# Patch-scan layer: part of the B products by ScalarE and TensorE, step sizes spread from DRAM, some C products on GpSimd

## The chip, the cores and the metric

The kernel runs on one core of a Trainium2 chip. All data are float32. The metric is the device time of one execution in microseconds. The core has a matrix engine (PE, with its weight loads shown apart as PEld), a vector engine (DVE), an activation engine (ACT), a general engine (POOL) and a queue that issues most of the transfers (SP). Each has its own list of instructions and works through it in order; they wait for one another by semaphores. Tiles lie in the on-chip memory SBUF or in PSUM, where PE writes its results; DRAM is off the chip.

## The reference

Four layers with residuals act on x of shape (8, 96, 64, 64). The change is in layer 2, a selective scan over patches. Cut to its core:

```python
xin, z = split(in_proj_w @ x)                 # 192 channels each
x_s = bilinear_sample(xin, ref + tanh(off2(gelu(bn(conv3x3(xin))))))
xt = patches of 4 x 4 pixels, L = 16 steps each
xs4 = [xt, xt turned, both reversed]          # 4 directions
dts, Bs, Cs = x_proj_weight @ xs4             # per direction; N = 16 states
delta = softplus(dt_projs @ dts + bias)
h[d, n] = h[d, n] * exp(delta[d] * A[d, n]) + delta[d] * u[d] * B[n]   # per step
y[d] = sum over n of h[d, n] * C[n]
y = layernorm(sum of the four directions + D * u) * silu(z)
x = x + out_proj_w @ y
```

Each channel d has 16 states n, so a recurrence runs for 192 x 16 rows, in each of four directions, over all pixels.

## The kernel before

**Tiling.** An image of 64 x 64 pixels is worked in eight chunks of 512 pixels (32 patches of 16 steps); eight images make 64 chunks. In a chunk, each of the four directions (in `ORDER`, index n = 0 to 3; n odd is a reversed one) has 12 groups: six sets of 32 channels, and two parts each. A group holds 32 channels x 4 states on 128 partitions, twice (two sets of states side by side), 1024 columns. So a chunk is 48 groups, and the layer 3072. Directions 0, 1 and 2, 3 form two pairs, which share one chain for delta.

**What one group needs** (class `WideSlots`, `slot`):
- L458: SP spreads delta and delta*u of 32 channels over 128 partitions, into a tile `dd` (512 KB). One spread serves the two parts. Before, it reads the SBUF tile `delta`, each channel's row going to four neighbouring partitions (`p = 4 * channel + state`).
- L466: ACT makes two exps of 512 columns, exp(delta * A), into the PSUM tile `ps_d` (`g.da`; three buffers).
- L485: POOL multiplies delta*u by B (`brep`) into the SBUF tile `dbu` (eight buffers): the B product, 1024 columns.
- L1584 (`scan`): DVE runs the recurrence over 1024 columns, from `ps_d` and `dbu` into `ps_d`.
- L490: DVE multiplies the states by C (`crep`) into `dbu`: the C product. A group listed in `LATE2` would have its scan write `dbu` and its C product done by POOL; the list is empty.
- L373 (`total`): PE sums over the states with a matrix of ones (`k_red2`), two matmuls of 512 columns (four instructions).

**Order.** The order on each engine is written out by hand, slot by slot: slot t holds scan t, the exps of group t+1, the C product of t-1, the B product of t+2, the sum of t-2 and the spread of t+6. Around these stand "side" instructions, put in a slot by `sl.at(slot, engine, run)`; "first" is ACT's place just after the exps, "act" its later place in the slot. A chunk begins at slot B, the next at B + 48, so the slots below are often given modulo 48. A pair begins at T = B or B + 24. Side work of a chunk begins 100 slots ahead of B: load, normalise, 3 x 3 convolution (18 taps), gelu, offsets, tanh, bilinear sampling on POOL (`lines` to `sampled`), the projections for u and for B and C, the softplus chain for delta (`pair`: L1495 to L1513 on ACT, L1522 to L1538 on POOL, 24 products of 512 columns per chunk), copies that mark the patch edges (`edges`, L1546). Behind the groups come centring, variance, gate (`gated`), output projection, residual, store (`end`, `gates`). All side matmuls share one PSUM tile, `ps_a`, which ACT empties before the next may begin.

Gelu (L1312), tanh (L1341) and silu (L1469) each need a table load on ACT, and one more to get back to the tables of exp and ln.

Of the kernel before, what the change touches and what calls it, by code (L numbers as in the profile page):

```python
# [13 lines left out]
ALU = mybir.AluOpType  # L14
# [43 lines left out]
def shape_constants():  # L58
# [19 lines left out]
    for d in range(GC2):  # L78
        red[d * HS2 : (d + 1) * HS2, 64 + d] = 1.0
# [33 lines left out]
def lay_out(i):  # L113
# [16 lines left out]
    for k in range(4):  # L130
# [28 lines left out]
        .transpose(2, 3, 0, 1, 4)  # L159
# [84 lines left out]
LOG_EXP = "natural_log_exp_and_others"  # L244
FAR = 1e25
AHEAD = 4
AHEAD2, SPREAD2 = 6, 4
LATE2 = ()
# [193 lines left out]
class WideSlots(Slots):  # L442


    def run(self):
        ts = list(self.plan) + [t + d for t in self.groups for d in (-self.ahead, 3)]
        with self.S.tc.manual_schedule():
            for t in range(min(ts), max(ts) + 1):
                self.slot(t)

    def slot(self, t):
# [4 lines left out]
        elif g:  # L456
# [3 lines left out]
                g.steps().unsqueeze(1).to_broadcast([self.gc, 128 // self.gc, 2 * NW]),  # L460
            )
        g = G(t + 1)
        if g:
            g.da = new(self.psd, [128, 2, NW], "ps_d")
            for i in range(2):
                nc.scalar.activation(  # L466
                    g.da[:, i, :], g.dd[:, 0, :], AF.Exp, scale=g.a[:, i : i + 1]
                )
        self.side(t, "first")
        g = G(t)  # L470
        if g:
            g.h = g.dbu if g.late else g.da
            g.scan(*(v.rearrange("p i l -> p (i l)") for v in (g.h, g.da, g.dbu)))
# [4 lines left out]
        g = G(t - 3)  # L478
# [4 lines left out]
        if g:  # L483
            g.dbu = new(self.pool, [128, 2, NW], "dbu", bufs=8)
            nc.gpsimd.tensor_tensor(  # L485
                g.dbu, g.dd[:, 1:2, :].to_broadcast([128, 2, NW]), g.b(), ALU.mult
            )
        g = G(t - 1)
        if g:
            (nc.gpsimd if g.late else nc.vector).tensor_tensor(g.dbu, g.h, g.c(), ALU.mult)  # L490
        for engine in ("pool", "dve", "sp", "end"):
# [698 lines left out]
def layer2(S, src, dst, st_in, st_out, images, cp, W, ready, finish):  # L1190
# [3 lines left out]
    with ExitStack() as ctx:  # L1194
# [32 lines left out]
        for k in range(4):  # L1227
# [3 lines left out]
        for k in range(2):  # L1231
            t = new(cp, [CH + 1, 2, NW], f"xs{k}")
# [11 lines left out]
        def front(ch, b, pad, xs, c, B):  # L1244
# [4 lines left out]
            def load():  # L1249
                ch["x"] = new(fp, [CH, 10 * IW], "xl")  # L1250
# [50 lines left out]
            for m, slots, last in (  # L1301
                (0, ((-81, 1), (-80, 2), (-79, 1), (-78, 1), (-77, 1), (-76, 1), (-75, 2)), -74),
                (1, ((-67, 1), (-66, 2), (-65, 1), (-64, 1), (-63, 1), (-62, 1), (-61, 2)), -60),
# [7 lines left out]
            def gelu():  # L1311
                nc.scalar.activation(ch["t"], ch["t"], AF.Gelu)  # L1312
                nc.scalar.preload_act_table_set(LOG_EXP)

            sl.at(B - 60, "act", gelu)

            def offset(a):
# [16 lines left out]
                sl.at(B - 59 + a, "pe", pe)  # L1334
                sl.at(B - 58 + a, "first", act)
# [4 lines left out]
            def tanh():  # L1340
                nc.scalar.activation(ch["f"], ch["f"], AF.Tanh)  # L1341
                nc.scalar.preload_act_table_set(LOG_EXP)

            def place():
# [3 lines left out]
                nc.scalar.activation(f, f, AF.Identity, bias=sl.half[:CH], scale=0.5)  # L1348

            sl.at(B - 57, "act", tanh)  # L1350
            sl.at(B - 56, "act", place)

# [28 lines left out]
            def sampled():  # L1381
                for k in range(2):
                    nc.gpsimd.tensor_tensor(
                        xs[:CH, 0, k * 256 : (k + 1) * 256].rearrange("p (n h w) -> p n h w", h=4, w=4),
# [11 lines left out]
            sl.at(B - 44, "act", lambda: nc.scalar.copy(xs[:CH, 1, :], turned(xs[:CH, 0, :])))  # L1396

            def inner(j):


                def pe():
# [4 lines left out]
                        xs[:CH, 0, :],  # L1406
# [9 lines left out]
                sl.at(B - 23 + j, "pe", pe)  # L1416
                sl.at(B - 22 + j, "first", act)
# [4 lines left out]
            def both():  # L1422
                ch["pa"] = new(psa, [128, NW], "ps_a")
                for o in range(2):
                    nc.tensor.matmul(
                        ch["pa"], bc_w[:, o].rearrange("c m s -> c (m s)"), xs[:CH, o, :],
                        start=o == 0, stop=o == 1,
                    )

            def both_out():  # L1430
                ch["bc"] = new(fp, [128, NW], "bc")
# [5 lines left out]

            sl.at(B - 20, "pe", both)
            sl.at(B - 19, "first", both_out)
            sl.at(B - 19, "sp", both_store)  # L1440

        def gates(ch, pad, T):
            x = pad[:, 1:9, 1 : IW + 1]

            def gate(m):
# [16 lines left out]
                sl.at(T + m, "pe", pe)  # L1462
                sl.at(T + 1 + m, "first", act)
# [8 lines left out]
            sl.at(T + 2, "act", silu)  # L1472

        def pair(ch, xs, n, T):
# [4 lines left out]
            def first(j):  # L1479
                def pe():  # L1480
# [5 lines left out]
                        xs[:, n, :],  # L1486
# [752 lines left out]
```

## Time and profile before

| what | us |
| --- | --- |
| median of 17 runs (18056.6 to 18186.87) | 18152.37 |
| the profiled execution | 18125.05 |
| its span, first to last instruction | 18123.2 |
| first and last scan of the patch layer, from the span's start | 3875.4, 14309.9 |

| engine | busy us in the span | share |
| --- | --- | --- |
| DVE | 16212.3 | 89% |
| POOL | 14803.3 | 82% |
| PE | 13711.7 | 76% |
| ACT | 10061.2 | 56% |

The span holds four layers: layer 0 to about 3050 us, layer 1 to about 3870, the patch layer to about 14310, layer 3 after it. Shares over the whole span mix them. Busy times are sums of the instructions' records; consecutive records of an engine overlap by about 0.1 us, so the distance from start to start is what adds up to time.

### The profile page before, as it was taken

The page shows a single profiled execution, that of the slowest core. Times are in us where ns is not written, and L with a number is a line of the kernel's source. Part 1 is how long each engine was busy: PE and PEld are TensorE (multiplying, and loading weights), DVE is VectorE, ACT ScalarE, POOL GpSimd, SP SyncE. Part 2 cuts the span into 40 slices and gives each one's busy share as a digit, 9 for nine tenths or more (in the row PEclk, how much of TensorE's full clock was granted, in tenths as well). Part 3 has the DMA queues.
Part 4 walks back from the last instruction along what each step waited for, and adds up shares of the span by engine and source line. Part 5 has one row for each costly group of instructions (what it writes and reads, how often), then busy time and mean ns, then how long its engine had stood idle before and what let it go on. Part 6 is the DMA issues. An engine that isn't in the chain of part 4 may idle for free. (4 is left out here: it accounts for less than half of the span.)

```text
span 18123.2 us, 125849 instructions
## 1 busy us (share of the span) xinstructions
PE 13711.7 (76%) x32964; PEld 4902.4 (27%) x32964; DVE 16212.3 (89%) x11111; ACT 10061.2 (56%) x16056; POOL 14803.3 (82%) x8876
## 2 busy tenths in 40 slices
PE   8999998968888888888888888888888644444433
PEld 2323223722222222222222222222222111111111
DVE  7999998679999999999999999999999766777667
ACT  6777775556666666666666666666666311111110
POOL 7999996059999999999999999999999656666555
PEclk8999998989999999999999999999999866666666
DMA  7888887366665666666566666656565444544444
GB/s 125 148 149 149 149 149 120 65 153 137 132 138 131 139 130 137 134 134 137 132 138 131 138 131 137 134 134 137 132 138 130 119 130 142 151 143 143 138 127 121
DMA packets 802719, 2437.25 MB, mean 134 GB/s; under 512 B 259123, under 2 KB 260864, under 8 KB 734830
## 3 DMA queue, kind: packets, MB, share of 16 engines
q1 hardware_dynamic: 654541, 1976.06, 52.3%
q0 software_dynamic: 147456, 453.13, 8.3%
q8 instruction: 262, 4.29, 0.1%
q14 instruction: 460, 3.76, 0.1%
HBM read 1116.39 MB, written 104.46 MB: 67 GB/s over the span
## 5 line engine op out<-in xcount | busy, mean ns | idle before, releaser
L373 PE MATMUL ps_y<-dbu,k_red 128*96 128x512 f32 x15360 | 7603.6, 620 | 1472.9 <-DVE dbu L490 1424.8
L485 POOL TENSOR_TENSOR dbu<-dd,brep 128x1024 f32<-128x1024 f32 x3072 | 7212.0, 2359 | 222.9 <-PE ps_y L373 105.9
L1584 DVE TENSOR_TENSOR_SCAN ps_d<-ps_d,dbu 128x1024 f32<-128x1024 f32 x3072 | 7015.7, 2284 | 126.9 <-issue 106.9
L466 ACT ACTIVATE ps_d<-dd,l_alog 128x512 f32<-128x512 f32 x6144 | 4241.6, 691 | 3353.0 <-DVE dbu L490 3236.4
L373 PEld LDWEIGHTS ps_y<-dbu,k_red 128*96 128x96 f32 x15360 | 2346.4, 166 | 6373.2 <-DVE dbu L490 3380.7
L490 DVE TENSOR_TENSOR dbu<-ps_d,crep 128x1024 f32<-128x1024 f32 x3072 | 3702.3, 1205 | 0.0
L2073 POOL DMA_INDIRECT v<-t,idx x2304 | 2191.9, 951 | 1541.5 <-DVE s L2100 705.1
L2100 DVE TENSOR_REDUCE s<-v 128x864 f32<-128x3456 f32 x256 | 1553.6, 6069 | 445.5 <-remote 236.6
L355 POOL TENSOR_TENSOR dbu<-dd,brep 128x1024 f32<-128x1024 f32 x768 | 1794.5, 2355 | 164.4 <-DMA dd<-delta 145.4
L2091 DVE TENSOR_TENSOR v<-v,ps_w 128x3456 f32<-128x3456 f32 x256 | 958.4, 3744 | 656.0 <-ACT ps_w L2083 584.7
L735 DVE TENSOR_TENSOR_SCAN ps_d<-ps_d,carry,dbu 128x512 f32<-128x512 f32 x1184 | 1452.8, 1272 | 96.4 <-POOL dbu L355 75.9
L1280 PE MATMUL ps_a<-pad,woff 96*96 96x512 f32 x2304 | 1146.5, 598 | 26.6 <-ACT pad L1257 24.1
L2119 ACT COPY smp<-ps_t 128x768 f32<-128x768 f32 (+1 forms) x512 | 244.5, 529 | 1659.1 <-remote 947.3
L337 ACT ACTIVATE ps_d<-dd,l_alog 128x512 f32<-128x512 f32 x1536 | 999.6, 682 | 182.7 <-DMA dd<-delta 126.3
L2111 PE MATMUL ps_t<-k_ident,s 128*128 128x128 f32 (+1 forms) x1792 | 326.9, 334 | 965.1 <-issue 571.6
L365 DVE TENSOR_TENSOR dbu<-ps_d,crep 128x512 f32<-128x512 f32 x1344 | 850.6, 674 | 0.0
L1522 POOL TENSOR_TENSOR sp_m<-sp_m,sp_s 128x512 f32<-128x512 f32 x384 | 487.8, 1271 | 371.8 <-ACT sp_s L1510 371.8
L1908 PE MATMUL ps_a<-xpad,l_om 96*27 96x512 f32 x1152 | 605.3, 674 | 53.8 <-issue 53.6
L1925 PE MATMUL ps_u<-k_ident,oc 27*128 27x27 f32 x256 | 32.8, 251 | 697.2 <-ACT oc L1920 577.6
L1280 PEld LDWEIGHTS ps_a<-pad,woff 96*96 96x96 f32 x2304 | 373.8, 164 | 668.0 <-issue 551.8
L2142 PE MATMUL ps_o<-smp,l_w 128*96 128x512 f32 (+1 forms) x896 | 477.6, 692 | 97.8 <-ACT smp L2119 91.8
L2111 PEld LDWEIGHTS ps_t<-k_ident,s 128*128 128x128 f32 (+1 forms) x1792 | 252.5, 170 | 1094.5 <-issue 875.8
(278 smaller groups left out, 15916.8 us busy)
## 6 DMA issues: line engine op xcount, KB each, us to landing
dd<-delta SPq DMA_DIRECT2D x2304, 512.0 KB
brep<-bcd SPq DMA_DIRECT2D x256, 1024.0 KB
crep<-bcd SPq DMA_DIRECT2D x256, 1024.0 KB
v<-t,idx POOLq DMA_INDIRECT x2304
xo<-x SPq DMA_DIRECT2D x128, 192.0 KB
x<-xo SPq DMA_DIRECT2D x128, 192.0 KB
bcd<-bc SPq DMA_DIRECT2D x64, 256.0 KB
xn<-x SPq DMA_DIRECT2D x64, 192.0 KB
```

The source lines that it names most:

```text
L337: nc.scalar.activation(da, g.dd[:, 0, :], AF.Exp, scale=g.a[:, i : i + 1])
L355: nc.gpsimd.tensor_tensor(g.dbu, g.dd[:, 1:2, :].to_broadcast([128, 2, NW]), g.b(), ALU.mult)
L373: self.S.nc.tensor.matmul(y, self.red[:, HD - self.gc * (g.n + 1) : 2 * HD - self.gc * (g.n + 1)], g.dbu[:, i, :], start=first and i == 0, ...
L466: nc.scalar.activation(g.da[:, i, :], g.dd[:, 0, :], AF.Exp, scale=g.a[:, i : i + 1])
L485: nc.gpsimd.tensor_tensor(g.dbu, g.dd[:, 1:2, :].to_broadcast([128, 2, NW]), g.b(), ALU.mult)
L490: (nc.gpsimd if g.late else nc.vector).tensor_tensor(g.dbu, g.h, g.c(), ALU.mult)
L735: nc.vector.tensor_tensor_scan(out, da, dbu, carry[:, n + i : n + i + 1] if c else 0.0, ALU.mult, ALU.add)
L1280: nc.tensor.matmul(ch["pk"][:HD, :], woff[:, k, m * HD : (m + 1) * HD], pad[:, dy : dy + 8, dx : dx + IW], start=k == 0, stop=k == KT - 1,)
L1584: nc.vector.tensor_tensor_scan(out[:, way], da[:, way], dbu[:, way], 0.0, ALU.mult, ALU.add)
L2073: nc.gpsimd.indirect_dma_start(out=st["v"][:, k].rearrange("p q c -> p (q c)"), out_offset=None, in_=flat, in_offset=bass.IndirectOffsetOn ...
L2091: nc.vector.tensor_tensor(v3, v3, ps_w[:, g % 2, j * 4 * KT : (j + 1) * 4 * KT] .unsqueeze(2) .to_broadcast([128, 4 * KT, CH]), ALU.mult,)
L2100: nc.vector.tensor_reduce(st["s"], st["v"].rearrange("p k q c -> p k c q"), mybir.AxisListType.X, ALU.add,)
```

## The change

1. **Layout.** The partition of a group becomes `p = 32 * state + channel` ("state by channel"): `k_red2`, `l2_alog`, the spreads of dd, brep and crep follow it.
2. **Delta through DRAM.** The tile delta | delta*u of a pair is stored in a DRAM tile `dud` in three parts (slots T-12, T-11, T-8), and the spreads read from there. `delta` has one buffer instead of two, and the tile `sp_m` is gone.
3. **B products by ScalarE.** For the groups of part 1 of each odd n (12 of 48), the second 512 columns of the B product are made in another way: delta*u is transposed by PE (`rows`, 16 transposes per chunk and pair together), so that the steps lie on partitions; B is transposed too (`over`, four); ACT multiplies by B as a scale column (`scaled`, 16 x 192 columns per pair); and PE transposes the products back into the second half of `ps_d`, four per group (`turn_of`). The exp that would have gone there goes to `dbu`, the POOL product is 512 columns, and the scan is two scans of 512.
4. **Late groups.** `LATE2` names five of the 48 groups; their C product is POOL's. It moves to slot t+2, the sum to t+4; all other side work of POOL now stands before it.
5. **Slots.** Side work is moved to make room: the projections for u and B, C earlier, the softplus chain three to four slots earlier, the output projection ten earlier; silu seven slots after its first gate matmul instead of two. Tanh uses a table set with exp and tanh (`EXP_TANH`), which saves one table load per chunk. The gates of the last chunk come at B + 50 instead of B + 42.
6. **Tiles.** Three `pad` buffers instead of four; the turned copy of `xs` is gone (matmuls read it turned); `bc` and `xo` share the buffer of `xl`.

The counts of instructions per chunk, before and after: scans of 1024 columns 48 and 36, of 512 columns 0 and 24; C products on DVE 48 and 43; B products of 1024 columns 48 and 36, of 512 columns 0 and 12; transposes 0 and 68; scalings 0 and 32; table loads 6 and 5; spreads of dd 24 and 24; stores to `dud` 0 and 6.

```diff
-LATE2 = ()
+LATE2 = (15, 18, 20, 38, 40)
...
-                g.steps().unsqueeze(1).to_broadcast([self.gc, 128 // self.gc, 2 * NW]),
+                g.steps().unsqueeze(0).to_broadcast([128 // self.gc, self.gc, 2 * NW]),
...
             for i in range(2):
-                nc.scalar.activation(
-                    g.da[:, i, :], g.dd[:, 0, :], AF.Exp, scale=g.a[:, i : i + 1]
-                )
+                da = g.dbu if g.turn and i else g.da
+                nc.scalar.activation(da[:, i, :], g.dd[:, 0, :], AF.Exp, scale=g.a[:, i : i + 1])
+            if g.turn:
+                g.turn(g.da[:, 1, :])
...
-            g.scan(*(v.rearrange("p i l -> p (i l)") for v in (g.h, g.da, g.dbu)))
+            if g.turn:
+                g.scan(g.h[:, 0, :], g.da[:, 0, :], g.dbu[:, 0, :])
+                g.scan(g.h[:, 1, :], g.dbu[:, 1, :], g.da[:, 1, :])
+            else:
+                g.scan(*(v.rearrange("p i l -> p (i l)") for v in (g.h, g.da, g.dbu)))
...
-        g = G(t - 3)
+        g = G(t - 4)
         if g and g.late:
             self.total(g)
...
+            n = 1 if g.turn else 2
             nc.gpsimd.tensor_tensor(
-                g.dbu, g.dd[:, 1:2, :].to_broadcast([128, 2, NW]), g.b(), ALU.mult
+                g.dbu[:, :n, :], g.dd[:, 1:2, :].to_broadcast([128, n, NW]), g.b()[:, :n, :],
+                ALU.mult,
             )
+        self.side(t, "pool")
+        g = G(t - 2)
+        if g and g.late:
+            nc.gpsimd.tensor_tensor(g.dbu, g.h, g.c(), ALU.mult)
         g = G(t - 1)
-        if g:
-            (nc.gpsimd if g.late else nc.vector).tensor_tensor(g.dbu, g.h, g.c(), ALU.mult)
+        if g and not g.late:
+            nc.vector.tensor_tensor(g.dbu, g.h, g.c(), ALU.mult)
...
-            sl.at(B - 60, "act", gelu)
+            sl.at(B - 58, "act", gelu)
...
+            def over():
+                ch["pa"] = new(psa, [128, NW], "ps_a")
+                for k in range(4):
+                    at = slice(k * 128, (k + 1) * 128)
+                    nc.tensor.transpose(ch["pa"][:, at], ch["bc"][:, at], S.ident)
...
-            sl.at(T + 2, "act", silu)
+            sl.at(T + 7, "act", silu)
...
+                def store():
+                    if j == 0:
+                        pr["rows"] = new(dp, [BLK * 128, 2 * NW], "dud")
+                    nc.sync.dma_start(
+                        pr["rows"][j * 128 : (j + 1) * 128],
+                        pr["d"][:, j].rearrange("p x l -> p (x l)"),
+                    )
+
+                sl.at(T - (12, 11, 8)[j], "act", edges)
+                sl.at(T - (12, 11, 8)[j], "sp", store)
...
+            def scaled(m):
+                def run():
+                    if m == 0:
+                        pr["prod"] = new(fp, [128, 4, 6, HS2, GC2], "prod")
+                    k, q = m // HS2, m % HS2
+                    nc.scalar.activation(
+                        pr["prod"][:, k, :, q, :],
+                        pr["du"][:, k, :].rearrange("p (g c) -> p g c", c=GC2),
+                        AF.Copy,
+                        scale=ch["bt"][:, k, n, q : q + 1],
+                    )
+
+                return run
+
+            m = 0
+            for t, count in (
+                (
+                    (-7, 2), (-4, 2), (-3, 2), (-2, 1), (-1, 1), (0, 1), (2, 1), (3, 3), (4, 1),
+                    (5, 2),
+                ),
+                ((-7, 3), (-6, 3), (-5, 3), (-4, 1), (-3, 1), (-2, 1), (3, 2), (4, 2)),
+            )[n]:
+                for _ in range(count):
+                    sl.at(T + t, "act", scaled(m))
+                    m += 1
...
+            def turn_of(h, g):
+                def run(out):
+                    for k in range(4):
+                        nc.tensor.transpose(
+                            out[:, k * 128 : (k + 1) * 128],
+                            pr["prod"][:, k, 3 * h + g].rearrange("p s c -> p (s c)"),
+                            S.ident,
+                        )
+
+                return run
...
+                        turn=turn_of(h, g) if n % 2 and part else None,
...
-                gates(ch, pad, B + (42 if b == images[-1] and c == NC - 1 else 61))
+                gates(ch, pad, B + 50)
```

## The prediction

> **What bounds the kernel now.** I read four views in this order: busy time by stretch (where does the changed layer lie, and which engine is full in it), the groups by line (what one slot costs), the timeline of one slot (how instructions overlap), and the list of waits (where the full engine still loses time).
>
> Busy time in 6 ms from the middle of the patch layer; the columns are length, then busy time and instruction count of PE, PEld, DVE, ACT and POOL, then granted clock, DMA share, GB/s:
>
> ```profile
> core 0: us, PE busy (x) PEld busy (x) DVE busy (x) ACT busy (x) POOL busy (x), PEclk, DMA share, GB/s
> 6000.00:12000.00 6000.00, 5068.12 (x10995) 1686.34 (x10994) 5934.81 (x3609) 4041.86 (x5826) 5651.76 (x3067) 0.99 0.60 134
> 1000.00:2500.00 1500.00, 1388.93 (x2894) 447.84 (x2892) 1429.33 (x1628) 1082.25 (x2163) 1392.11 (x611) 0.95 0.89 149
> ```
>
> DVE is busy 98.9%, POOL 94.2%, PE 84.5%, ACT 67.4%. The reader is to see that DVE sets the pace and that POOL is next.
>
> Groups by line, with shapes kept apart (busy us, mean ns | idle before):
>
> ```profile
> L373 PE MATMUL ps_y<-dbu,k_red 128*96 128x512 f32 x15360 | 7603.6, 620 | 1472.9 <-DVE dbu L490 1424.8 <-DVE dbu L365 34.1 <-POOL dbu L360 4.4
> L485 POOL TENSOR_TENSOR dbu<-dd,brep 128x1024 f32<-128x1024 f32 x3072 | 7212.0, 2359 | 222.9 <-PE ps_y L373 105.9 <-DMA dd<-delta 98.2 <-DVE ps_d L1584 14.2
> L1584 DVE TENSOR_TENSOR_SCAN ps_d<-ps_d,dbu 128x1024 f32<-128x1024 f32 x3072 | 7015.7, 2284 | 126.9 <-issue 106.9 <-POOL dbu L485 17.3
> L490 DVE TENSOR_TENSOR dbu<-ps_d,crep 128x1024 f32<-128x1024 f32 x3072 | 3702.3, 1205 | 0.0
> L735 DVE TENSOR_TENSOR_SCAN ps_d<-ps_d,carry,dbu 128x512 f32<-128x512 f32 x1184 | 1452.8, 1272 | 96.4 <-POOL dbu L355 75.9 <-ACT ps_d L337 16.5 <-ACT carry L744 2.1
> ...
> L1522 POOL TENSOR_TENSOR sp_m<-sp_m,sp_s 128x512 f32<-128x512 f32 x384 | 487.8, 1271 | 371.8 <-ACT sp_s L1510 371.8
> ...
> L735 DVE TENSOR_TENSOR_SCAN ps_d<-ps_d,dbu 128x512 f32<-128x512 f32 x160 | 186.5, 1210 | 94.1 <-POOL dbu L355 86.9 <-ACT ps_d L337 6.9
> ```
>
> A slot is one scan (2284) and one C product (1205) on DVE, one B product (2359) on POOL. The two L735 lines, from layer 0, show what half a scan costs.
>
> Timeline of DVE and of ACT where DVE stops (start us, length, then what; the bracket is idle time before):
>
> ```profile
> 9057.44 2.29 DVE L1584 TENSOR_TENSOR_SCAN ps_d<-ps_d,dbu 128x1024 f32<-128x1024 f32 x1
> 9059.63 1.21 DVE L490 TENSOR_TENSOR dbu<-ps_d,crep 128x1024 f32<-128x1024 f32 x1
> 9061.54 2.30 DVE L1584 TENSOR_TENSOR_SCAN ps_d<-ps_d,dbu 128x1024 f32<-128x1024 f32 x1 [0.70 <-issue]
> 9063.75 1.21 DVE L490 TENSOR_TENSOR dbu<-ps_d,crep 128x1024 f32<-128x1024 f32 x1
> ```
> ```profile
> 9055.60 0.76 ACT L1294 ACTIVATE off<-ps_a,sh,sc 96x512 f32<-96x512 f32 x1
> 9056.37 1.28 ACT L1312 ACT_TABLE_LOAD   x1
> 9057.67 1.06 ACT L1312 ACTIVATE off<-off 96x1024 f32<-96x1024 f32 x1
> 9058.74 1.28 ACT L1313 ACT_TABLE_LOAD   x1
> 9060.04 1.41 ACT L466 ACTIVATE ps_d<-dd,l_alog 128x512 f32<-128x512 f32 x2
> ```
>
> Start to start a scan takes 2.19 us and a product 1.125 us, so an undisturbed slot is 3.315 us. The stop of 0.70 us is called "issue", but ACT's exps for that scan ended just before it: behind gelu and its two table loads (3.67 us) they came late. Tanh and silu each stop DVE for 0.51 us in the same manner in this chunk. Over the layer the "issue" time of L1584 is 106.9/64 = 1.67 us per chunk.
>
> POOL's waits in the same 6 ms (total us, times, longest):
>
> ```profile
> POOL sp_m L1522 <- ACT sp_s L1510: 200.1, 69, 3.8
> POOL dbu L485 <- PE ps_y L373: 57.3, 63, 1.0
> POOL dbu L485 <- DMA dd<-delta: 56.0, 55, 2.0
> ```
>
> L1584's own view gives first and last start as 3875.4 and 14309.9 us: 10434 us for 64 chunks of 48 slots, 163.0 us a chunk. From the rows: 48 x 3.315 = 159.1, one gating product (1.12) and one statistic (0.60), 1.67 stops; sum 162.5, 0.5 short.
>
> **The change, per chunk, on DVE.** (a) Five late groups: their C product leaves DVE, 5 x 1.125 = -5.63 us. No bound is needed, the row is the instruction itself. (b) Twelve scans of 1024 become 24 of 512. No half scan without a carry operand in this layer is shown; layer 0's takes 1.210 (1.12 start to start, with the overlap of 0.09 seen above): 12 x (2.24 - 2.19) = +0.6. Upper bound, the carry form 1.272 (1.18): 12 x 0.17 = +2.0. Lower bound zero. I take +0.6, since the new scans have no carry. That one factor comes from PSUM and one from the product tile in either half, as now, is why I leave the rate alone. (c) The stops. Tanh shares a table set with exp now, so one table load goes (1.28 us) and its 3.67 us become 1.06 in one slot and 2.4 in the next: no stop. Silu moves three slots from its gate copy: from the exps in front of it to the end of the next exps is 1.35 + 3.67 + 1.42 + 0.2 = 6.64 us, and DVE's two slots there last 6.68: no stop. Gelu stands one slot behind the conv eviction, same 6.64, but in slot 39 group 38's product is gone from DVE, so the two slots last 3.32 + 2.24 = 5.56: a stop of 1.1. So 1.67 becomes 1.1: -0.55. Bounds: no stops at all, -1.67; the old ones and the new one, +1.1. Sum: -5.63 + 0.6 - 0.55 = -5.6 us.
>
> **Is anything else then the bound?** The new chunk would be 157.4 us.
> POOL: 0.942 x 163.0 = 153.6 busy. Twelve B products halve (2.32 start to start against 1.24 for the 512 form): -13.0. Five late products come, priced as the B product they resemble: +11.6. Result 152.2, 97% of 157.4. POOL's waits were 9.4 us a chunk (the lines above and 33 us of smaller ones, over 36.8 chunks); 5.2 are left. I count them at nothing because they are taken when POOL is ahead: in that state it waits for ACT's logarithm or for a product buffer. If that cover were gone, 152.2 + 9.4 = 161.6 would be the chunk. A late product in slot t waits for scan t-2, and the B product of t+3 stands behind it: it starts at the end of that scan, takes 2.32, and 2.32 more brings the next B product some 2 slots before its scan.
> PE: weight loads of 512-column passes follow each other every 0.43 us, so 299 instructions a chunk are at most 129 us. New are 12 x 4 transposes, 16 of delta*u and 4 of the B rows: 68. Layer 3's seven in a row (L2111) take 0.93 us, 0.133 each: +9 us, 138 of 157.4. In PE's queue the four of a slot stand ahead of the sum matmuls and of the side work. They may start when DVE's product two groups back frees the PSUM tile, and have 3.3 us plus a first half scan (1.12); the fullest stretch before them is slot 30 (sum, gated output, residual, tap and transposes: 4.9 us against 3.3), which leaves a lag of 1.6. Hidden; each microsecond by which the cover falls short costs 12 us a chunk.
> Transposes have a rule against them. The Trainium skill, TensorE: Matmul & The Clock Gate, Part 4: PE-mode transpose, gives about 275 ns for one in a kernel. By it the 68 would cost an estimated 18.7 us, and PE would be at 148 of 157.4: the same verdict with less room.
> ACT: 109.9 busy. 32 scalings of 192 elements: not in the trace; the 32-element copies L1546 follow each other at 0.24 us, the 512-element exps with a scale column (L466) at 0.675. Between them by size: 0.39, 12.5 us; bounds 7.7 and 21.6. Four evictions of delta*u and one of B, at or below a 512 eviction's 0.48: +2. Out: the turned copy L1396 (1.1) and a table load (1.28). Result 122, 78%. What hides it is ACT's 1.9 us of rest in a plain slot; three scalings in slots 17 to 19 make 1.35 + 0.48 + 1.17 = 3.0 of 3.3. At the upper bound they make 3.9, and with the short slots 19 and 21 stop DVE by some 1.5 us a chunk.
> SP and DMA: 24 spreads stay 24, now from DRAM; six stores of 512 KB are new. SP's stores wait for ACT's edge copies at T-12, -11, -8; behind them wait the spreads of T-4, T-2 and T. A spread that must wait for the store at T-8 is issued at T-6 and first used by POOL at T-2, four slots or 13 us later. Rates: in the layer-0 stretch spreads from SBUF fill 0.89 of the engines at 149 GB/s, 167 GB/s full; 12.6 MB a chunk at that are 75 of the 98 us (0.60 x 163) in this layer, so the other 9.2 MB of the 134 GB/s, mostly DRAM reads, took 23 us, 400 GB/s. Estimate after: 31 + 23 + 19 for the stores = 73 us. I take no gain and no loss: POOL's waits for dd were 1.5 us a chunk and hidden. If each spread came a microsecond too late, 24 us a chunk.
> The Trainium skill, DMA: Bandwidth & Descriptors, Anatomy of one DMA, speaks against the detour: some 2 us fixed per transfer, most of it the receipt of the write, heaviest in HBM. By it a store and a spread in series are an estimated 2 x 3.2 us; the page's sum is the same while 13 us cover them. No landing time is shown here.
>
> **Sum.** 64 x -5.6 = -358 us. At the front, 3866 to 3875, the first scan waits for the chain edge copy, spread, exp: store and reload come in, at the mean 134 GB/s 3.9 us each, less what the earlier slots give: +6. At the tail the last chunk's gates come eight slots later, after the last scan: two evictions and silu, +6. 18125 (profiled run; span 18123) - 358 + 12 = 17779; that run lies 27 under the median, so 17806, said as 17810 us (-1.9%).
>
> **Rivals.**
> 1. POOL becomes the bound: its old waits stay with it at late products and logarithms. 161.6 a chunk, -1.4 x 64 + 12: about 18075. For it: 97% busy, two engines tied to each other. Against: the waits named end on ACT and PE at points where POOL was ahead.
> 2. Slower: the split scan waits for its transposes. Place: second half scan of 12 groups, PE behind slots 30 to 36. It decides from 5.6/12 = 0.47 us a group. At 1 us: +6.4 a chunk, 18152 + 410 + 12 = 18575. For it: PE 88% and one ps_a buffer that chains PE to ACT. Against: 4.4 us of deadline, 1.6 of lag.
> 3. The DRAM detour and the earlier slots do nothing and the new stops (upper bounds of b, c and ACT: -5.63 + 2.0 + 1.1 + 1.5) eat most: -1.0 x 64 + 12: 18100.
>
> **How the numbers follow.** Forecast 0.62, with its own range 17700 (no stop left, half scans free: -7.3 x 64) to 17955 (half way to the upper bounds: b 1.3, c 0.3, ACT 0.75, so -3.3 x 64); rival 1: 0.14; rival 3: 0.10, of which 0.06 within 0.2% of before (36 us, about what a measurement of this kernel can tell from no change); rival 2: 0.14. Faster 0.62 + 0.14 + 0.04 = 0.80, same 0.06, slower 0.14. The range goes from 17700 up to the two small gains, 18080.
>
> **What would show it.** Right: 5 x 64 POOL products of dbu by crep at 2.3 us; half scans near 1.21; L1584's stops near 70 us in all; DVE still at 98% and POOL near 97%; patch layer near 10080 us; DMA share under 0.5. Wrong: DVE idle before the second half scan, put down to PE (rival 2); DVE idle with POOL never waiting (rival 1); half scans over 1.27; waits for dd grown.

## The result, and the profile after

| | median us | ratio to before, 95% interval |
| --- | --- | --- |
| before (47 runs beside it) | 18151.21 | 1 |
| after (8 runs, 21477.06 to 21558.3) | 21505.58 | 1.1855 [1.1842, 1.1868] |

The change makes the kernel 18.6% slower, where 1.9% faster was forecast. The profiled execution has a span of 21541.1 us. By the scan's own view the first and last scan of the patch layer start at 3878.3 and 17675.3 us: 215.6 us a chunk, against 163.0 before. 64 x 52.6 = 3366 us, of 3418 us between the two spans (18123.2 before): nearly all of the loss lies in the patch layer.

In the lines below, numbers such as L468 are lines of the kernel that left them, not of the kernel before. In the changed kernel L459 issues the spread of dd, L468 is an exp, L492 a B product, L1667 a scan and L502 a C product; in the kernels of the experiments they are shifted by a line or two.

The same 6 ms of the patch layer as in the prediction, busy time by engine, then PE's clock, the DMA share and GB/s:

```profile
6000.00:12000.00 6000.00, 4434.38 (x10186) 1696.75 (x10186) 4426.36 (x2922) 3314.83 (x5388) 4235.60 (x2454) 0.87 0.29 116
```

DVE is busy 73.8% (98.9% before), POOL 70.6% (94.2%). No engine is the bound any more, and the DMA engines are busy 29% of the time, half as much as before (60%). If nothing computes all the time and the transfers seem to have room, something waits for a transfer that is slow rather than big. What waits, in the same 6 ms (total us, times, longest):

```profile
ACT ps_d L468 <- DMA dd<-dud: 1702.7, 216, 12.2
POOL dbu L492 <- DMA dd<-dud: 1698.4, 270, 10.9
DVE ps_d L1667 <- POOL dbu L492: 1269.2, 284, 7.9
```

Before, POOL's wait for the spreads was 56.0 us in this window. Now the exps and the B products wait for them, and the scan waits for the B product. The chain of work that ended last, over the whole span and by engine (spreads of dd are 28 of the 37% of DMA), and two groups, where the idle time before them is the last column:

```profile
DMA 37%; PE 26%; DVE 11%; ACT 9%; another core or an unknown queue 9%; issue 7%; POOL 2%; SPq 0%; DVEq 0%; POOLq 0%; ACTq 0%
...
L492 POOL TENSOR_TENSOR dbu<-dd,brep 128x1024 f32<-128x1024 f32 (+1 forms) x3072 | 6387.2, 2086 | 4072.4 <-DMA dd<-dud 3867.8
...
L1667 DVE TENSOR_TENSOR_SCAN ps_d<-ps_d,dbu 128x1024 f32<-128x1024 f32 (+1 forms) x2752 | 5537.5, 2016 | 3127.2 <-POOL dbu L492 2960.8
```

Over half of the same chain from 9000 to 9300 us (52%) is single spreads, most of the rest work of PE; some of its longest pieces (start us, us, what):

```profile
9039.60 30.69 DMA dd<-dud
9072.91 32.65 DMA dd<-dud
...
9146.54 28.87 DMA dd<-dud
...
9186.00 24.68 DMA xl<-x
```

These spreads of 512 KB take some 30 us from issue to landing; the kernel asks for them six slots ahead, 20 us at the old pace. Even the load of x (192 KB) takes 25. In experiment 9 below, whose spreads have the old shape, the list of transfers gives 3.9 us at the median.

The trace also keeps each DMA packet with its start and length. From these I counted how many packets of SP's queue are in flight at once, from 6 to 12 ms:

```
share of the time with so many packets in flight
kernel                     none   4      5      15 and 16   median packet of 4 KB
before                     .27    .012   .010   .37         313 ns (source in SBUF)
after                      .005   .848   .069   .03         159 ns (source in DRAM)
```

For 85% of the time exactly four packets are in flight, hardly ever none. I take it that four engines share a transfer. A spread is 128 packets of 4 KB, so each of the four takes 32 of them, 5.1 us in all; the rest of its 30 us it would stand behind transfers issued earlier. 24 spreads a chunk x 32 x 159 ns = 122 us, and the eight wide transfers for brep and crep (128 packets of 8 KB, 309 ns) 8 x 32 x 309 ns = 79 us. The sum, 201 us, fills 93% of the 215.6 us chunk: by this reckoning the queue, four packets at a time, is the new bound, and experiments 1, 2 and 11 test it. The DMA row averages over sixteen engines, so four that are always busy look much like sixteen that are busy a quarter of the time.

The diff says where the four comes from: the spread's access pattern was [32, 4, 1024] and is [4, 32, 1024]; that of brep and crep [32, 4, 2048] and is [4, 32, 2048].

The Trainium skill has this rule, which the prediction did not use: DMA: Bandwidth & Descriptors, Rules for kernel authors, says that a transfer's engines are set by the slowest dimension of its access patterns, and that "a leading zero-stride broadcast of c copies" keeps the whole transfer to at most c engines. The count above agrees: four packets in flight, where a spread of dd has four copies outermost, and one of brep or crep four rows.

### The profile page after: what moved, and what is told of

The parts are those of the page before. It is cut to its first block, busy times and chain, and to the rows that moved or that the text cites. A ratio compares the mean times of both kernels' runs of the same rounds, so it can differ in the third digit from the quotient of the medians.

```text
span 21541.1 us, 137598 instructions
## 1 busy us (share of the span) xinstructions
PE 15064.9 (70%) x37316; PEld 5873.1 (27%) x37316; DVE 16070.3 (75%) x11559; ACT 10641.1 (49%) x18296; POOL 14717.1 (68%) x9195
## 4 chain that ended last, share of the span: by engine, by line
DMA 37%; PE 26%; DVE 11%; ACT 9%; another core or an unknown queue 9%; issue 7%; POOL 2%; SPq 0%; DVEq 0%; POOLq 0%; ACTq 0%
DMA dd<-dud 28%; PE ps_y L374 11%; DMA xl<-x 7%; DVE ps_d L1667 3%; PE ps_a L1292 3%; DVE dbu L502 3%; ACT ps_d L468 2%; PE ps_a L2003 2%; PE ps_k L649 1%; DMA dd<-delta 1%; DVE ps_d L747 1%; PE ps_a L1333 1%; POOL dbu L492 1%; PE ps_o L2237 1%
## 5 line engine op out<-in xcount | busy, mean ns | idle before, releaser
L492 POOL TENSOR_TENSOR dbu<-dd,brep 128x1024 f32<-128x1024 f32 (+1 forms) x3072 | 6387.2, 2086 | 4072.4 <-DMA dd<-dud 3867.8
L1667 DVE TENSOR_TENSOR_SCAN ps_d<-ps_d,dbu 128x1024 f32<-128x1024 f32 (+1 forms) x2752 | 5537.5, 2016 | 3127.2 <-POOL dbu L492 2960.8
L468 ACT ACTIVATE ps_d<-dd,l_alog 128x512 f32<-128x512 f32 x5376 | 3701.5, 689 | 5574.6 <-DMA dd<-dud 3927.3
L502 DVE TENSOR_TENSOR dbu<-ps_d,crep 128x1024 f32<-128x1024 f32 x2752 | 3322.2, 1207 | 299.9 <-DMA crep<-bcd 283.5
L356 POOL TENSOR_TENSOR dbu<-dd,brep 128x1024 f32<-128x1024 f32 x768 | 1793.5, 2356 | 130.5 <-DMA dd<-delta 114.1
L1693 PE MATMUL ps_d<-k_ident,prod 128*128 128x128 f32 x3072 | 567.1, 315 | 861.9 <-ACT ps_d L468 861.9
L338 ACT ACTIVATE ps_d<-dd,l_alog 128x512 f32<-128x512 f32 x1536 | 999.4, 682 | 153.8 <-DMA dd<-delta 99.6
L1667 DVE TENSOR_TENSOR_SCAN ps_d<-dbu,ps_d 128x512 f32<-128x512 f32 x704 | 865.1, 1229 | 74.3 <-ACT ps_d L468 1.4
L1620 ACT ACTIVATE prod<-turned,bt 128x192 f32<-128x192 f32 x2048 | 825.6, 446 | 0.0
L1693 PEld LDWEIGHTS ps_d<-k_ident,prod 128*128 128x128 f32 x3072 | 423.5, 162 | 1353.0 <-ACT ps_d L468 1162.4
L1667 DVE TENSOR_TENSOR_SCAN dbu<-ps_d,dbu 128x1024 f32<-128x1024 f32 (+1 forms) x320 | 660.3, 2063 | 144.0 <-ACT ps_d L468 141.6
L499 POOL TENSOR_TENSOR dbu<-dbu,crep 128x1024 f32<-128x1024 f32 x320 | 754.7, 2358 | 0.0
```

The source lines that it names most:

```text
L338: nc.scalar.activation(da, g.dd[:, 0, :], AF.Exp, scale=g.a[:, i : i + 1])
L356: nc.gpsimd.tensor_tensor(g.dbu, g.dd[:, 1:2, :].to_broadcast([128, 2, NW]), g.b(), ALU.mult)
L468: nc.scalar.activation(da[:, i, :], g.dd[:, 0, :], AF.Exp, scale=g.a[:, i : i + 1])
L492: nc.gpsimd.tensor_tensor(g.dbu[:, :n, :], g.dd[:, 1:2, :].to_broadcast([128, n, NW]), g.b()[:, :n, :], ALU.mult,)
L502: nc.vector.tensor_tensor(g.dbu, g.h, g.c(), ALU.mult)
L1667: nc.vector.tensor_tensor_scan(out[:, way], da[:, way], dbu[:, way], 0.0, ALU.mult, ALU.add)
```

## The experiments

Each compares with the kernel before on the same chip. The runs were made on several chips, and on that of the last three (17308 us before) layer 3 takes some 840 us less while the patch layer takes as long as elsewhere; so ratios and lengths of a chunk are compared, not microseconds across chips.

**1. Four transfers for each spread.** One for each state set of 32 partitions, so 32 is outermost again; the layout stays.

```diff
-            nc.sync.dma_start(
-                g.dd.rearrange("p x l -> p (x l)"),
-                g.steps().unsqueeze(0).to_broadcast([128 // self.gc, self.gc, 2 * NW]),
-            )
+            for s in range(128 // self.gc):
+                nc.sync.dma_start(
+                    g.dd[s * self.gc : (s + 1) * self.gc].rearrange("p x l -> p (x l)"),
+                    g.steps(),
+                )
```

and the same for brep and crep.

> Every spread of dd, brep and crep is issued as four transfers of 32 partitions, so that the outermost dimension of each is 32 in place of 4; the layout, the DRAM source and all else stay as in the changed kernel. Theory 1 (width): a spread whose outermost dimension is 4 is moved four packets at a time; the changed kernel's chunk of 215.6 us is 24 x 32 packets x 159 ns + 8 x 32 x 309 ns = 201 us of such transfers. Then the chunk falls to DVE's 157 to 160 us and the time to 17800 to 18000 us, with waits for dd under 3 us a chunk. Theory 2 (source): the spread is late because it reads rows that were just stored to DRAM, or because they come from DRAM at all. Then nothing changes: 21400 to 21600 us. More issues on SP (96 more a chunk at 0.5 us, 48 us of 157) may cost up to 100 us in either.

Measured: 18174.15 us, ratio 1.0018 [1.0007, 1.0029], a chunk 163.6 us. Four packets are no longer the rule (none 34%, sixteen 34% of the time). All of the loss is gone, as Theory 1 said, with the layout and the source unchanged; but none of the gain has come, and the time lies above Theory 1's range.

**2. The old layout with everything else of the change.** Partition = 4 * channel + state again.

```diff
-                g.steps().unsqueeze(0).to_broadcast([128 // self.gc, self.gc, 2 * NW]),
+                g.steps().unsqueeze(1).to_broadcast([self.gc, 128 // self.gc, 2 * NW]),
...
-                        pr["prod"][:, k, :, q, :],
+                        pr["prod"][:, k, :, :, q],
```

with `k_red2`, `l2_alog`, brep and crep as they were.

> The partition of a group is again 4 x channel + state, as before the change, so the spreads have an outermost dimension of 32 in one transfer each; delta still goes through DRAM, and the scaled products, the late groups and the slots are those of the changed kernel (ACT's products are written with a step of four). Theory 1 (width): 17750 to 18000 us, the forecast's 17810 if its sums for DVE hold. Theory 2 (source): still 21000 to 21600 us, since the DRAM source and its store stay.

Measured: 18161.02 us, ratio 1.0007 [0.9997, 1.0017], a chunk 163.07 us (163.03 before); again the loss is gone and the range of Theory 1 missed.

```profile
6000.00:12000.00 6000.00, 5369.40 (x13498) 2057.56 (x13497) 5791.32 (x3869) 4455.97 (x7108) 5602.42 (x3254) 0.97 0.43 154
```

The number of transfers is that of the changed kernel, so it is not their count or the detour through DRAM that cost, but the order of the dimensions. The DMA share falls from 0.60 to 0.43, although more bytes move. DVE's busy time falls by 2.4% (143 us in this window), and yet the chunk is no shorter: its stops grow from 64 to 168 us, and a gap that experiment 6 explains takes 42. This kernel is the base of experiments 5 to 10.

**3 and 4. Half of the repair.** Only dd in four transfers, only brep and crep in four.

> Only the spreads of dd are issued as four transfers of 32 partitions; brep and crep keep the outermost dimension of 4. Theory 1 (width): four at a time for brep and crep are 8 x 9.9 = 79 us a chunk and dd at sixteen at a time 24 x 1.3 = 31 us, 110 us together with 19 for stores: under 157, so about as fast as with all split, at most 150 us over it. Theory 2 (source): 21400 to 21600 us.

> Only the spreads of brep and crep are issued as four transfers; dd keeps the outermost dimension of 4. Theory 1 (width): dd 24 x 5.1 = 122 us a chunk and brep, crep 8 x 2.5 = 20, with stores and the rest about 155 to 165 us a chunk in one queue, so transfers and DVE are about level: 18100 to 18900 us, between the changed kernel and the split of dd. Theory 2 (source): 21400 to 21600 us.

Measured: 20913.91 us, 1.1518 [1.1495, 1.1542], with dd alone; 19160.2 us, 1.056 [1.0542, 1.0577], with brep and crep alone. Both expectations were missed. Alone the two repairs take back 0.034 and 0.130 of the 0.185; both at once (experiment 1) take back all of it. What SP's queue waited for (total us, times, longest) in 6 ms of the kernel with dd split:

```profile
SPq L460 <- DMA brep<-bcd: 1470.9, 116, 16.2
SPq L460 <- DMA crep<-bcd: 1318.3, 116, 13.6
```

and of the one with brep and crep split:

```profile
SPq L1653 <- DMA dd<-dud: 1095.7, 267, 7.3
```

Quick and slow transfers share one queue, and the quick ones' issue stands behind the slow ones' end: 46% of the time in the first case. Four packets in flight are still 41% and 60% of the time. By the packets' sum the wide transfers (79 us a chunk) should cost less than the spreads (122 us), and it is the other way round: with them alone the chunk is (17104.2 - 3886.4) / 64 = 206.5 us, with the spreads alone (15330.3 - 3880.1) / 64 = 178.9. My reading, which no run tests, is that what counts is how long the queue behind a transfer stands, and a wide one is 1 MB in one piece. Why SP waits for a transfer that its next instruction doesn't need, the trace does not say.

**5. No late groups.** On the old layout, `LATE2 = ()`.

> As the kernel with the old layout (18161 us), but no group is late: all 48 C products are DVE's again. Theory A (DVE still sets the pace; what the late groups gain is eaten by the split scans and by new stops): DVE gets 5 x 1.125 = 5.6 us a chunk back, the stop behind gelu shrinks from 1.6 to about 0.7, so 163.1 becomes 166 to 168 and the time 18350 to 18520 us. Theory B (POOL sets the pace at 97%, as the first rival had it): POOL loses 11.6 us a chunk, and the time stays or falls, 17900 to 18160 us.

Measured: 18301.92 us, 1.008 [1.0063, 1.0097]; first and last scan 3875.6 and 14444.7, a chunk 165.1. That is slower, as Theory A said, though less so than its range; Theory B is out. The five late groups are worth 165.1 - 163.07 = 2.0 us a chunk, not 5.63. The other 3.6 are stops: DVE's are 168 us in 6 ms of experiment 2, 4.6 us a chunk, and 35 us here, 1.0 a chunk, nearly all in two lines and none behind POOL:

```profile
DVE ps_d L1667 <- ACT ps_d L468: 17.6, 37, 0.5
DVE ps_d L1667 <- PE ps_d L1693: 16.8, 15, 1.3
```

**6. The C product between the two half scans.**

```diff
                 g.scan(g.h[:, 0, :], g.da[:, 0, :], g.dbu[:, 0, :])
-                g.scan(g.h[:, 1, :], g.dbu[:, 1, :], g.da[:, 1, :])
...
             nc.vector.tensor_tensor(g.dbu, g.h, g.c(), ALU.mult)
+        g = G(t)
+        if g and g.turn:
+            g.scan(g.h[:, 1, :], g.dbu[:, 1, :], g.da[:, 1, :])
```

> As the kernel with the old layout (18161 us), but the second half scan of a split group is issued after the C product of the group before, not straight behind the first half. In the trace the second half starts 0.10 us after the first ends, where other neighbours on DVE overlap by 0.09. Theory A (the second half waits for the end of the first, on the same engine, so a split scan costs 0.26 us more than a whole one): 11 x 0.2 = 2.1 us a chunk go, 64 x 2.1 = 135 us, 18000 to 18050 us; pairs of halves then cost 2.24. Theory B (the halves are slow by their operands, one factor from PSUM and the other from SBUF): no gain, 18140 to 18180 us.

Measured: 18024.31 us, 0.9926 [0.991, 0.9943], a chunk (14145.9 - 3873.3) / 64 = 160.5 us, as expected of Theory A. The timeline of DVE (start us, us) in experiment 2, with the halves side by side:

```profile
9038.12 1.21 DVE L502 TENSOR_TENSOR dbu<-ps_d,crep 128x1024 f32<-128x1024 f32 x1
9039.25 1.22 DVE L1667 TENSOR_TENSOR_SCAN ps_d<-ps_d,dbu 128x512 f32<-128x512 f32 x1
9040.57 1.23 DVE L1667 TENSOR_TENSOR_SCAN ps_d<-dbu,ps_d 128x512 f32<-128x512 f32 x1
9041.70 1.21 DVE L502 TENSOR_TENSOR dbu<-ps_d,crep 128x1024 f32<-128x1024 f32 x1
...
9150.45 1.21 DVE L1667 TENSOR_TENSOR_SCAN dbu<-ps_d,dbu 128x512 f32<-128x512 f32 x1
9151.58 1.20 DVE L1667 TENSOR_TENSOR_SCAN dbu<-dbu,ps_d 128x512 f32<-128x512 f32 x1
```

and here, with the product of the group before in between:

```profile
9039.00 1.22 DVE L1669 TENSOR_TENSOR_SCAN ps_d<-ps_d,dbu 128x512 f32<-128x512 f32 x1
9040.13 1.21 DVE L501 TENSOR_TENSOR dbu<-ps_d,crep 128x1024 f32<-128x1024 f32 x1
9041.25 1.22 DVE L1669 TENSOR_TENSOR_SCAN ps_d<-dbu,ps_d 128x512 f32<-128x512 f32 x1
9042.37 2.27 DVE L1669 TENSOR_TENSOR_SCAN ps_d<-ps_d,dbu 128x1024 f32<-128x1024 f32 x1
```

Side by side, the second half starts 0.10 us after the first has ended, where other neighbours on DVE overlap by 0.08 to 0.09; in the trace DVE waits for a semaphore of its own until the first half is done. The pair takes 2.45 us from start to start, a whole scan 2.19: +0.26. With another instruction between them the overlap is back, each step 1.12 to 1.13. That the halves write one tile is not the whole reason: the pair of the late group (the last two lines of experiment 2) writes both halves into one `dbu` and overlaps by 0.08. Why only halves written to `ps_d` wait is not shown.

The product comes in between in nine groups of a chunk; two others follow a late group, have no product to put there and stay as they were. Nine times 0.21 is 1.9 us a chunk, and the stops fell from 4.6 to 4.1; 2.6 came.

**7. The logarithm before the y copies.** Two copies of y on ACT (slots 25 and 49), which wait for PE's sums, go behind the softplus logarithm.

```diff
-            sl.at(B + 25, "act", rows(1))
+            sl.at(B + 25, "end", rows(1))
...
-                sl.at(B + 37 + 12 * h, "act", act)
+                sl.at(B + 37 + 12 * h, "end" if h else "act", act)
```

> As the kernel with the old layout (18161 us), but in the two slots where the logarithm of softplus stands behind ACT's copy of a finished y (which waits for PE's last sum), the copy is moved to the end of the slot. Theory A (DVE's stops named after POOL, 84 us in 6 ms or 2.3 us a chunk, come from that copy: the softplus sum on POOL waits for the logarithm, and the B product stands behind it in POOL's queue): these stops go, 1.5 to 2.3 us a chunk, 18010 to 18070 us. Theory B (POOL is late because it is full): the stops stay, 18140 to 18180 us.

Measured: 18113.23 us, 0.9974 [0.9964, 0.9984], a chunk 162.3: 0.8 us shorter, half of the least that Theory A expected, and between the two ranges. DVE's stops behind a POOL instruction fell from 84 to 35 us in 6 ms, but its stop at the gelu grew from 57 to 78. The reason for the edit, a stop of 1.33 us in experiment 2 (the bracket is idle time before the instruction):

```profile
9022.61 0.58 ACT L1719 COPY yy<-ps_y 96x512 f32<-96x512 f32 x1 [3.17 <-PE ps_y L374]
9023.09 1.48 ACT L1538 ACTIVATE sp_s<-sp_w 128x1536 f32<-128x1536 f32 x1
9024.65 1.26 POOL L1551 TENSOR_TENSOR delta<-delta,sp_s 128x512 f32<-128x512 f32 x1 [4.99 <-DVE dbu L502]
9025.88 2.36 POOL L492 TENSOR_TENSOR dbu<-dd,brep 128x1024 f32<-128x1024 f32 x1
9025.97 2.30 DVE L1667 TENSOR_TENSOR_SCAN ps_d<-ps_d,dbu 128x1024 f32<-128x1024 f32 x1 [1.33 <-POOL delta L1551]
```

It is read from the bottom: the scan waits for POOL, whose sum waited for ACT's logarithm, which stood behind a copy that waited 3.17 us for PE. (For POOL the view names a DVE product, which ended at 9024.63, just before. But in each of the seven waits of this sum from 9000 to 9600 us it starts 0.08 us after the logarithm's end, here at 9024.57, while the last DVE product ended anything from 0.02 to 1.63 us earlier.)

**8. Both edits, and late group 38 moved to slot 4.** `LATE2 = (4, 15, 18, 20, 40)`.

> The two edits before together, and the late group 38, whose missing product shortens DVE's slot while ACT is behind gelu's table loads, is replaced by group 4. Theory A: 163.1 - 2.1 (halves) - 2.0 (logarithm) - 1.5 (gelu) = 157.5 a chunk, 17750 to 17850 us, which is where the forecast's sum lay and better than both kernels. If POOL (152 of 157.5 us) sets the pace instead, 17900 to 18050 us.

Measured: 18018.32 us, 0.9924 [0.9907, 0.994], a chunk 160.8, level with experiment 6: Theory A is missed, and the time lies in the range of the alternative, in which POOL sets the pace (it is busy 95% of the 6 ms). DVE's two largest stops:

```profile
DVE ps_d L1669 <- POOL bl_bot L1390: 81.0, 32, 2.6
DVE dbu L1669 <- ACT ps_d L468: 49.5, 37, 1.4
```

The second is the stop at the gelu. It is not gone but smaller, 82 us in experiment 6 and 50 here: putting DVE's product back into that slot saves some 0.9 us a chunk of 2.3, not 1.5. The first, DVE behind the sampling product on POOL (`bl_bot`), was 17 us and has eaten the gain.

**9 and 10. Sampling one slot later; and one late group less.** To experiment 7's and 6's edits: POOL's sampling steps of slots -52 to -46 go to -51 to -45; in the tenth `LATE2 = (15, 18, 20, 40)` besides.

> The old partition order with the second half scan after the C product, the two y copies behind the logarithm, and the sampling steps of GpSimd one slot later than the B products' rows; late groups as in the change. Theory A (VectorE's stops set the time, and GpSimd's wait for ScalarE's fr, about 1.35 us a chunk, is what the logarithm's move uncovered): the gains of the two edits add, 18024 less 30 to 90, so 17930 to 18000. Theory B (GpSimd, busy 94 to 95% of the stage, has no slack left, so each stop taken from one slot comes back in another): level with the interleaving alone, 18010 to 18040, with a stop behind a GpSimd product that was not there before.

> The kernel with the sampling steps moved, but the late C product of slot 38 (beside the gelu) goes back to VectorE. Theory A: VectorE gets one product of 1.13 us a chunk back (+72 us) and the stop at the gelu falls from about 2.1 to 0.5 us a chunk (-100 us): within 40 us of the kernel with five late groups, rather below it. Theory B (GpSimd has no slack): GpSimd is freed of 2.36 us a chunk, and the stops behind its products fall as well, so 40 to 90 us faster than with five late groups.

Measured: 17220.5 us, 0.9949 [0.9932, 0.9965], a chunk 161.55; and 17270.19 us, 0.9977 [0.9968, 0.9987], a chunk 162.2; before on this chip 17308.19. DVE's stops in 6 ms of the ninth:

```profile
DVE dbu L1669 <- ACT ps_d L468: 85.2, 36, 2.5
DVE ps_d L1669 <- POOL dbu L491: 55.3, 35, 2.0
```

and of the tenth, with a wait of POOL:

```profile
DVE ps_d L1669 <- POOL dbu L491: 68.7, 35, 2.5
DVE dbu L1669 <- ACT ps_d L468: 53.9, 36, 1.6
...
POOL dbu L491 <- DMA dd<-dud: 101.5, 24, 6.3
```

The ninth is 1 us a chunk longer than experiment 6 alone: the gains of the two edits do not add, and Theory A is out. The stop behind the sampling is gone in both kernels, and one behind the B product is there, which experiment 6 hardly had (0.3 us). So much Theory B said, which expected the ninth level with experiment 6. The tenth is 50 us slower than the ninth, where Theory A allowed 40 and Theory B expected 40 to 90 faster. POOL has 2.36 us a chunk less to do in it, and DVE waits for POOL more, not less: POOL waits for the spreads itself, 101.5 us in 6 ms against 7.9 in the ninth. Neither theory holds for both kernels. The stop at the gelu gives 31 us back in 37 chunks, 0.85 a chunk, less than the 1.12 that the product costs.

**11. Several transfers for each spread, each still with 4 outermost.** On the changed kernel; two for dd, four for brep and crep, cut along the row.

```diff
-                g.steps().unsqueeze(0).to_broadcast([128 // self.gc, self.gc, 2 * NW]),
...
+            for x in range(2):
...
+                    g.steps()[:, x * NW : (x + 1) * NW]
+                    .unsqueeze(0)
+                    .to_broadcast([128 // self.gc, self.gc, NW]),
```

> The changed kernel with each spread issued as several transfers, as in the first experiment, but cut along the row and not by channel group: two for dd, four each for brep and crep, every one still 4 rows of channel groups outermost with 32 partitions in each. Theory A (a transfer keeps as many DMA engines at work as its outermost dimension counts, and these are the same few for each): the number of transfers does nothing, exactly 4 packets stay in flight for most of the time, the time stays at 21300 to 21900. Theory B (the first experiment won because several transfers were in flight at once, whatever their shape): 8 or 16 packets in flight, 18100 to 18700.

Measured: 20941.77 us against 17305.14, ratio 1.21 [1.2065, 1.2135]; first and last scan 3877.9 and 17934.6, a chunk 219.6 us.

```profile
6000.00:12000.00 6000.00, 4464.19 (x10029) 1689.73 (x10028) 4332.31 (x2874) 3249.42 (x5273) 4162.99 (x2416) 0.87 0.30 114
```

Exactly four packets are in flight for 76% of the time, five for 16%, sixteen for 2%. The time's own range of the expectation was for the other chip; by the chunk it is as slow as the changed kernel, and 4 us more. Here more transfers did nothing while each had four as its outermost dimension: together they still have four packets in flight. Theory A.

That they share the same four engines is what the Trainium skill says (DMA: Bandwidth & Descriptors, Why a DMA increments its semaphore by 16 and not by 1: a transfer issued by SP runs on the lowest-numbered engines); which engines they are, no run here shows.

The best version, experiments 6 and 8 (level within their intervals), is 0.75% faster than before: the old partition order, the detour, and the C product between the halves.

## Why the prediction was wrong

**The step that failed** is "24 spreads stay 24, now from DRAM ... I take no gain and no loss", with its sum 31 + 23 + 19 = 73 us of a chunk. It prices the spreads at the rate of all sixteen engines. The diff's new shape of the spread was listed as a layout and never costed. The prediction's own figures would have done: it takes 400 GB/s for DRAM reads on sixteen engines; at four of them that is 100 GB/s, and the 24 x 0.52 + 8 x 1.05 = 21 MB of a chunk take an estimated 210 us. The chunk measured 215.6. The bound it did name, 24 us for spreads a microsecond late, was too small by half: they came (215.6 - 163.0) / 24 = 2.2 us late each.

The detour itself was priced rightly. In experiment 2 stores and spreads from DRAM cost nothing that the chunk shows, and the DMA share fell to 0.43, as "DMA share under 0.5" had it; 0.43 of 163 us is 70, where the sum had 73. Landing times, which the prediction could not show, stand in experiment 9: 2.9 us for a store and 3.9 for a spread at the median, where it estimated 3.9 from its rows and 3.2 from the page's figure.

**With that put right the gain would still not have come.** The forecast for DVE was -5.63 + 0.6 - 0.55 = -5.6 us a chunk; experiment 2 has +0.04. By its terms:

- (a) late groups, "-5.63 ... No bound is needed, the row is the instruction itself". The instructions did go (320 POOL products of 2365 ns), but experiment 5 prices the whole exchange at 2.0 us. The rest comes back as stops that the late groups bring, 4.6 us a chunk with them against 1.0 without. I read them so: the exps of the group behind a late one have less cover, and POOL's queue is longer. An instruction's row is the bound of what taking it away can give, not its price.
- (b) split scans, +0.6 with 2.0 as upper bound. The half scan is 1.22 to 1.23 us where 1.21 was taken; but the overlap of 0.09 was assumed between two halves of which the second waits for the first. Measured 2.45 for the pair: 11 x 0.26, and 0.07 for the one late pair, +2.9 a chunk, outside the bounds. Experiment 6 shows this term by taking most of it away.
- (c) stops, 1.67 to 1.1. In experiment 2 they are, over 36.8 chunks:

```profile
DVE ps_d L1667 <- POOL delta L1551: 57.8, 37, 3.0
DVE dbu L1667 <- ACT ps_d L468: 57.3, 36, 1.6
DVE ps_d L1667 <- POOL bl_bot L1388: 26.3, 15, 2.9
DVE ps_d L1667 <- PE ps_d L1693: 19.1, 20, 1.1
```

With 8 us of smaller ones 168 us, 4.6 a chunk: +2.9. Tanh and silu no longer stop DVE, as forecast; gelu does with 1.56 (forecast 1.1, put down to the missing product in slot 39; with that product back, in experiments 8 and 10, 1.3 to 1.5 of 2.3 remain, so the cover was counted too long as well). The two POOL lines, 2.3 a chunk, were not forecast: "POOL's waits ... 5.2 are left. I count them at nothing because they are taken when POOL is ahead". In the stop shown at experiment 7 POOL was not ahead: the logarithm came late.

-5.63 + 2.9 + 2.9 = +0.2, against +0.04 measured.

**Other engines.** Over the chunk of experiment 2 POOL is busy 152.3 us (forecast 152.2), ACT 121.1 (122), PE 145.9, 8.2 more than before (forecast +9 for the 68 transposes; its total of 138 started from 129 where the busy time before was 137.7). Four transposes of a group follow each other every 0.13 us, as layer 3's row had it, and the estimate of 18.7 us for the 68 was too high: the 275 ns, which the skill gives for bf16, is close to one record here (273 ns), but such records overlap. Scalings of 192 elements in a row follow each other every 0.35 us in the changed kernel and 0.43 in experiment 2 (forecast 0.39, upper bound 0.675).

**Rivals.** None had the transfers. Rival 2 (transposes late, from 0.47 us a group) is wrong: the stops behind PE are 0.52 us in a whole chunk. It is the first half scan that waits there, not the second as the prediction thought. Rival 1 (POOL) is wrong for the changed kernel; in experiments 2 and 6 to 10 POOL is busy 92 to 95%, and a quarter to three fifths of DVE's stops end on it, but experiment 10 shows that its busy time alone does not set the chunk. Rival 3 (new stops eat the gain) is what the repaired kernel does, 60 us beyond its price.

Open: why experiment 10's spreads come late to POOL, why SP's issues wait for transfers before them, and why halves written to `ps_d` wait where those written to `dbu` do not.

## What to carry to other kernels

When a change reorders a layout, write down the access pattern of every transfer it touches, and look at the outermost dimension before the bytes: here one of four kept four packets in flight, and the DMA share of 0.29 showed room that was not there. Count packets in flight, or compare the time from issue to landing with the bytes. Price an instruction taken from a queue that has 1% of slack by what stands ready behind it, and put something independent between two halves of a split instruction.

## What the runs showed of the hardware

- A 4 KB packet of a spread took 313 ns at the median from SBUF (before) and 159 ns from DRAM, in experiment 2 too, where the spread has the shape of before. The source is not all: in experiment 1, also from DRAM, the median is 262 ns with sixteen or more packets in flight for half of the time.
- On DVE the second half scan into `ps_d` starts 0.10 us after the end of the first; other neighbours, and the late group's halves into `dbu`, start 0.08 to 0.09 before the end of the one ahead.
- ACT's scaling took 626 ns with an output step of four elements and 446 with none.
- PE's granted clock in the patch layer is 0.87 in the changed kernel, with PE busy 74%, 0.97 in experiment 2, with 89%, and 0.99 before, with 84.5%. The sums' matmuls of 512 columns are longer in the changed kernel (649 ns against 620 before), without being the bound. The busy share alone does not set the clock: experiment 4 has 0.94 with PE busy 85%, where the kernel before has 0.99.
